# A depthwise convolution stage regrouped: eight channels per tile, shared zero gaps between images, kernel rows in a ring of their own

## The chip, the cores and the metric

The kernel runs on one core of a Trainium2 chip. The metric is the device time of one execution in microseconds (us). All data is float32.

## The reference

Four layers work one after the other on a batch of 8 images with 384 channels and 32 x 32 pixels. The first two are Mamba blocks (projections, a short convolution, a recurrent scan, a gate), the second with a pooled attention gate and a two-layer perceptron behind it. The last two are what this change is about:

```python
# layer 2: seven depthwise convolutions (13x13, and smaller ones, some dilated), each with a batch norm, summed
out = bn_eval(dwconv(x, w_lk, 1), ...)
for i, (w, r) in enumerate(zip(branch_ws, dilates)):
    out = out + bn_eval(dwconv(x, w, r), ...)
# layer 3: a pointwise convolution, then a 13x13 depthwise one
y = jnp.einsum('bchw,oc->bohw', x, pw_w)
x_pw = bn(y, pw_g, pw_b, pw_m, pw_v) + x
out = bn(dwconv(x_pw, dwk_w), ...) + bn(x_pw * dw1_w, ...)
return gelu(out, approximate=False)
```

The kernel folds the seven branches of layer 2 into one 13 x 13 kernel per channel, and the two terms at the end of layer 3 into another. So each of the last two layers has one depthwise 13 x 13 convolution over 8 images of 32 x 32 in 384 channels.

## The kernel before, in words

`layers` (lines 224 to 929) computes both Mamba layers and the perceptron. Its order is written out as a plan with a slot for each step, under a manual schedule for all five engines. While it runs, `prepare` folds the convolution kernels and writes them to DRAM as tables `k2` and `k3`, in a form in which each row of a banded matrix is a window of 512 bytes into a longer line of padded kernel values. The perceptron leaves its result in the DRAM tensor `x3`: `mlp_out` (line 714) adds bias and residual into the tile `rows_out`, whose rows have zeros around the 32 pixels, and `mlp_store` (line 721) stores it, 128 channels at a time.

The tail then has three stages, `conv.run` on `x3`, `point.run` and `conv.run` again (lines 1078 to 1084). Here the scheduler of the framework places the instructions in program order on each engine, and adds the waits.

`Depthwise` does a convolution as matmuls with banded matrices. A group is 4 channels; there are 96 groups in a convolution. The 128 partitions of the image tile `xp` are 4 blocks of 32 image rows: the block number is a shift of the row by 0, 1, 2 or 3 columns. A row holds the 8 images side by side, each with 6 zeros to its left and 6 to its right (WIDE = 44, so 352 values). The tile `wt` holds, for each channel, the banded kernel matrices. For each channel, 4 matmuls of 128 x 32 weights by 256 columns (8 images of 32 pixels), each shifted by 4 columns more, sum up the 13 kernel columns. The 4 channels of a group write 4 different blocks of 32 partitions of one PSUM tile `ps`. The trace records two matmuls for each one in the program, so a group is 32 records.

For each group, `run` does the following:

- `load` (line 951) of the group 6 ahead: two image loads on GpSimd's queue (line 958), which bring the unshifted block for two of the channels and the block shifted by 2 for the other two; and four loads of kernel windows (line 962), two on SyncE's queue, one on ScalarE's and one on GpSimd's. There are 8 buffers each of `wt` and `xp`, and a buffer can be loaded again once the matmuls of its last group are done.
- four copies on VectorE, which make the other shifted blocks: line 975 twice (shift by 1), lines 976 and 977 (shift by 2, down and up).
- 16 matmuls (line 982), one activation with the bias on ScalarE (line 987, Identity in the first convolution and Gelu in the second), and the store of the result on ScalarE's queue (line 988).

In the built program every DMA that SyncE or ScalarE issues uses one of eight completion counters in rotation, and waits until the DMA that had the same counter before has landed. Before the change a group issues four of these (three kernel loads and the store), so a store waits for the store of two groups earlier. GpSimd's DMAs have eight counters of their own.

`Pointwise` (line 991) runs 16 steps of 512 columns: it loads `xt`, does 9 matmuls (line 1016), activations, an addition (line 1021), and stores to `x5` (line 1026) through the tiles `q_out`, again with zeros around the pixels.

Of the kernel before, what the change touches and what calls it, by code (L numbers as in the profile page):

```python
# [9 lines left out]
F32 = mybir.dt.float32  # L10
# [6 lines left out]
P = 128  # L17
B = 8
# [7 lines left out]
T = 512  # L26
NU = B * L // T
HW = 32
# [4 lines left out]
HK = 64  # L33
KP = 4
PAD = KS // 2
WIDE = HW + 2 * PAD
NG = C // 4
EPS = 1e-5
PAST = 16100
# [27 lines left out]
class Plan:  # L67
# [3 lines left out]
    def __init__(self):  # L71
        self.slots = {}
# [859 lines left out]
class Depthwise:  # L932
# [3 lines left out]

    NB, AHEAD = 8, 6

    def __init__(self, tc, st):
        nc = self.nc = tc.nc
        self.keep = st.enter_context(tc.tile_pool(name="d_keep", bufs=1, reuse_waits="tile"))
        self.work = st.enter_context(tc.tile_pool(name="d_work", bufs=4, reuse_waits="tile"))
        self.psum = st.enter_context(tc.tile_pool(name="d_ps", bufs=4, space=PSUM, reuse_waits="tile"))
        self.wts = [self.keep.tile([P, 4, HW, KP], F32, name=f"wt{i}") for i in range(self.NB)]
        self.xps = [self.keep.tile([P, 4, B * WIDE], F32, name=f"xp{i}") for i in range(self.NB)]
        for t in self.wts + self.xps:
            nc.gpsimd.memset(t, 0.0)

    def load(self, g, src, table):
        nc, n = self.nc, B * WIDE
        wt, xp = self.wts[g % self.NB], self.xps[g % self.NB]
        for h in range(2):
            rows = bass.AP(
                src.tensor, src.offset + (g * P + 2 * HW * h) * n + 2 * h, [[n, HW], [HW * n, 2], [1, n - 2 * h]]
            )
            nc.gpsimd.dma_start(xp[2 * HW * h : 2 * HW * h + HW, 2 * h : 2 * h + 2, 0 : n - 2 * h], rows)  # L958
        for s, queue in enumerate((nc.sync, nc.scalar, nc.sync, nc.gpsimd)):
            at = table.offset + (16 * g + s) * HK * KP  # L960
            windows = bass.AP(table.tensor, at, [[KP, HW], [4 * HK * KP, 4], [1, HW * KP]])
            queue.dma_start(wt[HW * s : HW * (s + 1)].rearrange("p q r j -> p q (r j)"), windows)  # L962

    def run(self, src, table, bias, func, store):
        nc = self.nc
        n = B * WIDE
        for g in range(self.AHEAD):
            self.load(g, src, table)
        for g in range(NG):
            wt, xp = self.wts[g % self.NB], self.xps[g % self.NB]  # L970
            if g + self.AHEAD < NG:
                self.load(g + self.AHEAD, src, table)
            for h in range(2):
                low, q = 2 * HW * h, slice(2 * h, 2 * h + 2)
                nc.vector.tensor_copy(xp[low + HW : low + 2 * HW, q, 0 : n - 1], xp[low : low + HW, q, 1:n])  # L975
            nc.vector.tensor_copy(xp[2 * HW :, 0:2, 0 : n - 2], xp[: 2 * HW, 0:2, 2:n])
            nc.vector.tensor_copy(xp[: 2 * HW, 2:4, 2:n], xp[2 * HW :, 2:4, 0 : n - 2])  # L977
            ps = self.psum.tile([P, T], F32, tag="ps", name="ps")
            x = xp.rearrange("p q (b c) -> p q b c", c=WIDE)
            for j in range(KP):  # L980
                for q in range(4):
                    nc.tensor.matmul(  # L982
                        ps[HW * q : HW * (q + 1), : B * HW], wt[:, q, :, j], x[:, q, :, 4 * j : 4 * j + HW],
                        start=j == 0, stop=j == KP - 1,
                    )
            o = self.work.tile([P, B, HW], F32, tag="o", name="o")
            nc.scalar.activation(o, ps[:, : B * HW], func, bias=bias[:, g : g + 1])
            nc.scalar.dma_start(store(g), o)


class Pointwise:


    NB = 3
# [37 lines left out]
def network(ctx: ExitStack, tc: tile.TileContext, a: dict, out: bass.AP):  # L1032
    nc = tc.nc
# [27 lines left out]
    x4 = dram.tile([C, HW * B * HW], F32, name="x4")  # L1061
# [3 lines left out]
    got = {"b2": const.tile([P, NG], F32, name="b2"), "b3": const.tile([P, NG], F32, name="b3")}  # L1065
# [3 lines left out]
    with ExitStack() as st:  # L1069

        past = st.enter_context(tc.tile_pool(name="past", bufs=1, reuse_waits="tile"))
        past.tile([P, PAST], F32, name="past")
        past_ps = st.enter_context(tc.tile_pool(name="past_ps", bufs=1, space=PSUM, reuse_waits="tile"))
        past_ps.tile([P, 4 * T], F32, name="past_ps")
        conv = Depthwise(tc, st)
        point = Pointwise(tc, st, conv.psum, a["pw"])
        x4_rows = x4.rearrange("c (r n) -> (c r) n", r=HW)
# [120 lines left out]
```

## Time and profile before

| what | value |
|---|---|
| median of 3 runs | 6941.13 us (6929.37 to 6941.44) |
| time of the profiled execution | 6954.78 us |
| span of its trace | 6952.9 us |
| mean granted TensorE clock | 0.926 |
| PE busy | 5904.4 us (85%) |
| VectorE busy | 5851.6 us (84%) |
| ScalarE busy | 4475.0 us (64%) |
| GpSimd busy | 5429.7 us (78%) |
| DMA, over the span | 1169.60 MB, mean 168 GB/s |

In the trace, times run from the span's start. The layers take it up to 6373 us, when the last `rows_out` is done. The first depthwise convolution then runs until 6595 us, the pointwise stage until 6732 us (its last store has landed), and the second convolution to the end at 6952.9 us. So what the change edits is some 580 us out of 6953 us, one twelfth.

Views used below: the table of busy time by stretches of the span gives, for each engine, busy time and in brackets the number of records, then the granted clock, the DMA share and the DMA rate. The DMA share is the mean busy share of the core's 16 DMA engines, summed over packets, so it can pass 1 where packets overlap. The table of instruction groups gives line, engine, operation, tiles, shapes and count, then busy time and the mean time in ns of one, then the idle time before them and what ended it. The table of waits says which instruction waited for which, in total, how often, and at most.

### The profile page before, as it was taken

The page shows a single profiled execution, that of the slowest core. Times are in us where ns is not written, and L with a number is a line of the kernel's source. Part 1 is how long each engine was busy: PE and PEld are TensorE (multiplying, and loading weights), DVE is VectorE, ACT ScalarE, POOL GpSimd, SP SyncE. Part 2 cuts the span into 40 slices and gives each one's busy share as a digit, 9 for nine tenths or more (in the row PEclk, how much of TensorE's full clock was granted, in tenths as well). Part 3 has the DMA queues.
Part 4 walks back from the last instruction along what each step waited for, and adds up shares of the span by engine and source line. Part 5 has one row for each costly group of instructions (what it writes and reads, how often), then busy time and mean ns, then how long its engine had stood idle before and what let it go on. Part 6 is the DMA issues. An engine that isn't in the chain of part 4 may idle for free. (4 is left out here: it accounts for less than half of the span.)

```text
span 6952.9 us, 78464 instructions
## 1 busy us (share of the span) xinstructions
PE 5904.4 (85%) x22562; PEld 2097.6 (30%) x22562; DVE 5851.6 (84%) x4975; ACT 4475.0 (64%) x7478; POOL 5429.7 (78%) x3146
## 2 busy tenths in 40 slices
PE   6777788888888888888888888888889889877898
PEld 2222222222322232222222232223223223324645
DVE  2899998999889888888889988988888998863849
ACT  4776666767676767767676767676677667742222
POOL 2888888888788878888888878887877888754626
PEclk7888898999999999999999999999999889999999
DMA  4665555666666566666666665656666666645979
GB/s 123 166 176 155 154 160 149 167 168 173 171 165 181 157 169 167 161 168 167 167 165 172 167 174 161 176 155 174 165 157 168 160 171 172 161 108 131 264 224 242
DMA packets 960565, 1169.60 MB, mean 168 GB/s; under 512 B 314057, under 2 KB 552713, under 8 KB 960137
## 3 DMA queue, kind: packets, MB, share of 16 engines
q1 hardware_dynamic: 787848, 1062.39, 57.5%
q10 hardware_dynamic: 147712, 55.08, 3.1%
q0 software_dynamic: 24576, 47.12, 2.3%
q8 instruction: 184, 3.01, 0.2%
q14 instruction: 245, 2.00, 0.1%
HBM read 909.39 MB, written 204.21 MB: 160 GB/s over the span
## 5 line engine op out<-in xcount | busy, mean ns | idle before, releaser
L532 POOL TENSOR_TENSOR dbu<-B,ru 128x1024 f32<-128x1024 f32 x1536 | 3584.9, 2357 | 136.9 <-DMA B<-bc 56.8
L525 ACT ACTIVATE h<-rd,A 128x512 f32<-128x512 f32 x3072 | 2117.5, 691 | 861.8 <-DVE hc L561 524.8
L553 DVE TENSOR_TENSOR_SCAN h<-h,state,dbu 128x512 f32<-128x512 f32 x1152 | 1482.4, 1287 | 221.1 <-ACT h L525 79.6
L561 DVE TENSOR_TENSOR hc<-h,C 128x1024 f32<-128x1024 f32 x1152 | 1410.8, 1225 | 129.2 <-PE acc L583 14.5
L556 DVE TENSOR_TENSOR_SCAN h<-h,dbu 128x1024 f32<-128x1024 f32 x576 | 1318.1, 2288 | 239.0 <-ACT h L525 182.4
L572 POOL TENSOR_TENSOR hc<-dbu,C 128x1024 f32<-128x1024 f32 x384 | 903.5, 2353 | 736.7 <-DVE dbu L556 337.1
L583 PE MATMUL acc<-hc,fold 128*32 128x512 f32 x6144 | 1174.6, 663 | 340.7 <-DVE hc L561 257.9
L415 PE MATMUL mm<-xt,wi 128*128 128x512 f32 x2232 | 1123.3, 642 | 43.6 <-ACT delta L491 18.9
L695 PE MATMUL f<-mx,wi 128*128 128x512 f32 x1152 | 610.5, 638 | 139.9 <-ACT fh L699 111.0
L708 PE MATMUL f<-fh,wo 128*128 128x512 f32 x1152 | 587.0, 628 | 82.0 <-DMA wo<-in_fc_dram 66.8
L415 PEld LDWEIGHTS mm<-xt,wi 128*128 128x128 f32 x2232 | 424.7, 202 | 745.4 <-issue 447.8
L604 PE MATMUL mm<-u,wo 128*128 128x512 f32 x1152 | 579.4, 643 | 38.5 <-DMA wo<-in_l_out_dram 31.4
L583 PEld LDWEIGHTS acc<-hc,fold 128*32 128x32 f32 x6144 | 165.9, 112 | 1163.7 <-DVE hc L561 548.5
L553 DVE TENSOR_TENSOR_SCAN dbu<-h,state,dbu 128x512 f32<-128x512 f32 x384 | 470.4, 1267 | 14.0 <-ACT h L525 8.6
L556 DVE TENSOR_TENSOR_SCAN dbu<-h,dbu 128x1024 f32<-128x1024 f32 x192 | 437.9, 2281 | 39.8 <-ACT h L525 29.3
L439 PE MATMUL mm<-xp,taps 128*64 128x512 f32 x1536 | 407.0, 653 | 33.8 <-DMA xp<-xp 12.4
L982 PE MATMUL ps<-xp,wt 128*32 128x256 f32 x6144 | 376.1, 387 | 66.0 <-DVE xp L977 30.3
L958 POOL DMA_DIRECT2D xp<-x x384 | 215.4, 565 | 276.8 <-DMA x<-q_out 139.8
L305 ACT ACT_TABLE_LOAD x289 | 370.8, 1283 | 5.9 <-PEq L1186 0.7
L695 PEld LDWEIGHTS f<-mx,wi 128*128 128x128 f32 x1152 | 209.3, 196 | 499.4 <-issue 248.5
L580 PE MATMUL acc<-u,skip 128*128 128x512 f32 x384 | 226.8, 675 | 153.7 <-DVE u L588 153.5
L425 ACT ACTIVATE xp<-mm,b_in 64x512 f32<-64x512 f32 x384 | 261.5, 681 | 140.8 <-PE mm L415 138.3
(152 smaller groups left out, 5876.2 us busy)
## 6 DMA issues: line engine op xcount, KB each, us to landing
ru<-uu SPq DMA_DIRECT2D x1536, 128.0 KB
rd<-dd SPq DMA_DIRECT2D x1536, 128.0 KB
wi<-w_in SPq DMA_DIRECT2D x372, 192.0 KB
xp<-xp SPq DMA_DIRECT2D x384, 128.5 KB
dd<-delta SPq DMA_DIRECT2D x192, 256.0 KB
uu<-delta SPq DMA_DIRECT2D x192, 256.0 KB
wo<-in_l_out_dram SPq DMA_DIRECT2D x96, 384.0 KB
wi<-fc_w SPq DMA_DIRECT2D x192, 192.0 KB
```

Source lines behind the costliest of these rows:

```text
L415: nc.tensor.matmul(s.ps[m], w[:, c], s.xt[:, c], start=c == 0, stop=c == KC - 1)
L439: nc.tensor.matmul(s.ps[d][64 * h : 64 * h + 64], taps[:, h, j], xp[h][:, 2 * j : 2 * j + T], start=j == 0, stop=j == 1,)
L525: nc.scalar.activation(y[:, q], s.dr[d][1][h][:, q], AF.Exp, scale=s.layer.A[:, at : at + 1])
L532: nc.gpsimd.tensor_tensor(dbu, s.B[g].unsqueeze(1).to_broadcast([P, 2, T]), s.ur[d][1][h], ALU.mult)
L553: nc.vector.tensor_tensor_scan(to[:, q], y[:, q], dbu[:, q], first, ALU.mult, ALU.add)
L556: nc.vector.tensor_tensor_scan(flat_to, flat_y, flat_b, first, ALU.mult, ALU.add)
L561: nc.vector.tensor_tensor(hc, to, s.C[g].unsqueeze(1).to_broadcast([P, 2, T]), ALU.mult)
L572: nc.gpsimd.tensor_tensor(hc, y, s.C[g].unsqueeze(1).to_broadcast([P, 2, T]), ALU.mult)
L583: nc.tensor.matmul(s.acc[d][32 * r : 32 * r + 32], k["fold"], tiles[r // 2][:, r % 2], start=False, stop=n == PER - 2)
L604: nc.tensor.matmul(s.ps[m], w[:, d], s.us[d], start=d == 0, stop=d == KD - 1)
L695: nc.tensor.matmul(s.ps[m], s.w["in", m][:, c], s.xt[:, c], start=c == 0, stop=c == KC - 1)
L708: nc.tensor.matmul(s.down, s.w["out", 2 * m + f // KD][:, f % KD], s.hs[f], start=f == 0, stop=f == KF - 1)
```

## The change

- A group is 8 channels, and a convolution has 48 groups. `xp` is 128 x 8 rows, with 4 buffers instead of 8, loaded 3 groups ahead instead of 6. Each group still has two image loads and four VectorE copies, now over 4 channels each instead of 2.
- Two images share one gap of 6 zeros (WIDE = 38, so a row has 304 values instead of 352), and 12 zeros stand behind the last image. `x3`, `x5`, `rows_out` and `q_out` shrink with it.
- `wt` is 128 x 8 x 128 values in a ring of its own with 11 buffers. The first 10 groups of each convolution are loaded by `early`, all on GpSimd's queue: for the first convolution right after the image tiles have been zeroed, for the second right after the first convolution. In the loop, the group 10 ahead is loaded, on SyncE (three of the four loads) and ScalarE (one).
- The zeroing of `wt` goes.
- Each group has two PSUM tiles, each with 16 matmuls, an activation and a store as before. The number of matmuls, activations and stores does not change.

```diff
-WIDE = HW + 2 * PAD
+WIDE = HW + PAD
...
-    NB, AHEAD = 8, 6
+    N2 = NG // 2
+    NB, AHEAD = 4, 3
+    NK, EARLY = 11, 10
...
-        self.wts = [self.keep.tile([P, 4, HW, KP], F32, name=f"wt{i}") for i in range(self.NB)]
-        self.xps = [self.keep.tile([P, 4, B * WIDE], F32, name=f"xp{i}") for i in range(self.NB)]
-        for t in self.wts + self.xps:
+        self.wts = [self.keep.tile([P, 8, HW, KP], F32, name=f"wt{i}") for i in range(self.NK)]
+        self.xps = [self.keep.tile([P, 8, B * WIDE + 2 * PAD], F32, name=f"xp{i}") for i in range(self.NB)]
+        for t in self.xps:
             nc.gpsimd.memset(t, 0.0)
-    def load(self, g, src, table):
+    def kernels(self, g, table, queues):
+        wt = self.wts[g % self.NK]
+        for s, queue in enumerate(queues):
+            at = table.offset + (32 * g + s) * HK * KP
+            windows = bass.AP(table.tensor, at, [[KP, HW], [4 * HK * KP, 8], [1, HW * KP]])
+            queue.dma_start(wt[HW * s : HW * (s + 1)].rearrange("p q r j -> p q (r j)"), windows)
+    def early(self, table):
+        for g in range(self.EARLY):
+            self.kernels(g, table, [self.nc.gpsimd] * 4)
+    def images(self, g, src):
         nc, n = self.nc, B * WIDE
-        wt, xp = self.wts[g % self.NB], self.xps[g % self.NB]
+        xp = self.xps[g % self.NB]
         for h in range(2):
             rows = bass.AP(
-                src.tensor, src.offset + (g * P + 2 * HW * h) * n + 2 * h, [[n, HW], [HW * n, 2], [1, n - 2 * h]]
+                src.tensor, src.offset + (2 * g * P + 4 * HW * h) * n + 2 * h, [[n, HW], [HW * n, 4], [1, n - 2 * h]]
             )
-            nc.gpsimd.dma_start(xp[2 * HW * h : 2 * HW * h + HW, 2 * h : 2 * h + 2, 0 : n - 2 * h], rows)
-        for s, queue in enumerate((nc.sync, nc.scalar, nc.sync, nc.gpsimd)):
-            ...
+            nc.gpsimd.dma_start(xp[2 * HW * h : 2 * HW * h + HW, 4 * h : 4 * h + 4, 0 : n - 2 * h], rows)
     def run(self, src, table, bias, func, store):
         for g in range(self.AHEAD):
-            self.load(g, src, table)
-        for g in range(NG):
+            self.images(g, src)
+        for g in range(self.N2):
-            if g + self.AHEAD < NG:
-                self.load(g + self.AHEAD, src, table)
+            if g + self.AHEAD < self.N2:
+                self.images(g + self.AHEAD, src)
+            if g + self.EARLY < self.N2:
+                self.kernels(g + self.EARLY, table, (nc.sync, nc.scalar, nc.sync, nc.sync))
             for h in range(2):
-                low, q = 2 * HW * h, slice(2 * h, 2 * h + 2)
+                low, q = 2 * HW * h, slice(4 * h, 4 * h + 4)
                 nc.vector.tensor_copy(xp[low + HW : low + 2 * HW, q, 0 : n - 1], xp[low : low + HW, q, 1:n])
-            nc.vector.tensor_copy(xp[2 * HW :, 0:2, 0 : n - 2], xp[: 2 * HW, 0:2, 2:n])
-            nc.vector.tensor_copy(xp[: 2 * HW, 2:4, 2:n], xp[2 * HW :, 2:4, 0 : n - 2])
-            ps = self.psum.tile([P, T], F32, tag="ps", name="ps")
-            ...
+            nc.vector.tensor_copy(xp[2 * HW :, 0:4, 0 : n - 2], xp[: 2 * HW, 0:4, 2:n])
+            nc.vector.tensor_copy(xp[: 2 * HW, 4:8, 2:n], xp[2 * HW :, 4:8, 0 : n - 2])
+            for a in range(2):
+                ps = self.psum.tile([P, T], F32, tag="ps", name="ps")
+                ...
+                nc.scalar.activation(o, ps[:, : B * HW], func, bias=bias[:, 2 * g + a : 2 * g + a + 1])
+                nc.scalar.dma_start(store(2 * g + a), o)
...
         conv = Depthwise(tc, st)
+        conv.early(got["k2"])
         point = Pointwise(tc, st, conv.psum, a["pw"])
         conv.run(
             x3, got["k2"], got["b2"], AF.Identity,
...
+        conv.early(got["k3"])
         point.run(x4, x5, got["pw"][:, 0:KC], got["pw"][:, KC:])
```

In the built program before and after, the instructions of `layers` stand in the same order; only the stores from `rows_out` are smaller. On ScalarE's queue in the loop, the kernel load of a group stands between the second activation of a group and its store.

More of the change, by code (lines that the diff above doesn't have):

```diff
@@ L945, in __init__ @@
         self.psum = st.enter_context(tc.tile_pool(name="d_ps", bufs=4, space=PSUM, reuse_waits="tile"))
-        self.wts = [self.keep.tile([P, 4, HW, KP], F32, name=f"wt{i}") for i in range(self.NB)]
-        self.xps = [self.keep.tile([P, 4, B * WIDE], F32, name=f"xp{i}") for i in range(self.NB)]
-        for t in self.wts + self.xps:
+        self.wts = [self.keep.tile([P, 8, HW, KP], F32, name=f"wt{i}") for i in range(self.NK)]
+        self.xps = [self.keep.tile([P, 8, B * WIDE + 2 * PAD], F32, name=f"xp{i}") for i in range(self.NB)]
+        for t in self.xps:
             nc.gpsimd.memset(t, 0.0)
-    def load(self, g, src, table):
+    def kernels(self, g, table, queues):
[8 more added lines that the diff above has]
+    def images(self, g, src):
         nc, n = self.nc, B * WIDE
-        wt, xp = self.wts[g % self.NB], self.xps[g % self.NB]
+        xp = self.xps[g % self.NB]
         for h in range(2):
             rows = bass.AP(
-                src.tensor, src.offset + (g * P + 2 * HW * h) * n + 2 * h, [[n, HW], [HW * n, 2], [1, n - 2 * h]]
+                src.tensor, src.offset + (2 * g * P + 4 * HW * h) * n + 2 * h, [[n, HW], [HW * n, 4], [1, n - 2 * h]]
             )
-            nc.gpsimd.dma_start(xp[2 * HW * h : 2 * HW * h + HW, 2 * h : 2 * h + 2, 0 : n - 2 * h], rows)
-        for s, queue in enumerate((nc.sync, nc.scalar, nc.sync, nc.gpsimd)):
-            at = table.offset + (16 * g + s) * HK * KP
-            windows = bass.AP(table.tensor, at, [[KP, HW], [4 * HK * KP, 4], [1, HW * KP]])
-            queue.dma_start(wt[HW * s : HW * (s + 1)].rearrange("p q r j -> p q (r j)"), windows)
+            nc.gpsimd.dma_start(xp[2 * HW * h : 2 * HW * h + HW, 4 * h : 4 * h + 4, 0 : n - 2 * h], rows)
     def run(self, src, table, bias, func, store):
@@ L967, in run @@
         for g in range(self.AHEAD):
-            self.load(g, src, table)
-        for g in range(NG):
-            wt, xp = self.wts[g % self.NB], self.xps[g % self.NB]
-            if g + self.AHEAD < NG:
-                self.load(g + self.AHEAD, src, table)
+            self.images(g, src)
+        for g in range(self.N2):
+            wt, xp = self.wts[g % self.NK], self.xps[g % self.NB]
+            if g + self.AHEAD < self.N2:
+                self.images(g + self.AHEAD, src)
+            if g + self.EARLY < self.N2:
+                self.kernels(g + self.EARLY, table, (nc.sync, nc.scalar, nc.sync, nc.sync))
@@ L979, in run @@
[L979 to L987, printed above, removed]
@@ L988, in run @@
-            nc.scalar.dma_start(store(g), o)
+            nc.vector.tensor_copy(xp[2 * HW :, 0:4, 0 : n - 2], xp[: 2 * HW, 0:4, 2:n])
+            nc.vector.tensor_copy(xp[: 2 * HW, 4:8, 2:n], xp[2 * HW :, 4:8, 0 : n - 2])
+            for a in range(2):
+                ps = self.psum.tile([P, T], F32, tag="ps", name="ps")
+                for j in range(KP):
+                    x = xp[:, :, 4 * j : 4 * j + n].rearrange("p q (b c) -> p q b c", c=WIDE)
+                    for q in range(4):
+                        c = 4 * a + q
+                        nc.tensor.matmul(
+                            ps[HW * q : HW * (q + 1), : B * HW], wt[:, c, :, j], x[:, c, :, 0:HW],
+                            start=j == 0, stop=j == KP - 1,
+                        )
+                o = self.work.tile([P, B, HW], F32, tag="o", name="o")
+                nc.scalar.activation(o, ps[:, : B * HW], func, bias=bias[:, 2 * g + a : 2 * g + a + 1])
+                nc.scalar.dma_start(store(2 * g + a), o)
@@ L1075, in network @@
         conv = Depthwise(tc, st)
+        x4_rows = x4.rearrange("c (r n) -> (c r) n", r=HW)
+        conv.early(got["k2"])
         point = Pointwise(tc, st, conv.psum, a["pw"])
-        x4_rows = x4.rearrange("c (r n) -> (c r) n", r=HW)
         conv.run(
```

## The prediction

> **What bounds the tail now.** I read the table of busy time by stretches first, to separate the stages:
>
> ```profile
> core 0: us, PE busy (x) PEld busy (x) DVE busy (x) ACT busy (x) POOL busy (x), PEclk, DMA share, GB/s
> 6500.00:6540.00 40.00, 36.24 (x610) 27.91 (x601) 37.65 (x73) 9.02 (x19) 32.47 (x57) 1.00 0.95 272
> ...
> 6640.00:6690.00 50.00, 50.00 (x118) 22.09 (x117) 13.17 (x19) 15.29 (x20) 0.00 (x0) 1.00 0.72 237
> ...
> 6860.00:6900.00 40.00, 35.37 (x580) 21.01 (x576) 37.65 (x73) 8.54 (x18) 30.09 (x54) 1.00 1.08 257
> ```
>
> In both convolutions (first and last line) VectorE does 73 copies in 40 us, one every 0.548 us: busy 94% of the time, the rest being the gap of 0.03 us between copies. The DMA share is about 1 there too. The pointwise stage (middle) is bound by TensorE. The groups on VectorE in the first convolution (busy us, mean ns of one, idle before them):
>
> ```profile
> L975 DVE COPY xp<-xp 32x702 f32<-32x702 f32 x192 | 99.9, 520 | 9.1 <-PE ps L982 3.1
> L977 DVE COPY xp<-xp 64x700 f32<-64x700 f32 x96 | 50.2, 523 | 3.3
> L976 DVE COPY xp<-xp 64x700 f32<-64x700 f32 x96 | 50.1, 522 | 3.3
> ```
>
> 384 copies of 702 or 700 values with almost no idle time: 4 x 0.548 = 2.19 us for 4 channels, 96 times 210 us. In the timeline they run from 6373.28 to 6589.1 (215.8 us), in the second convolution from 6734.08 to 6946.9 (212.8 us). TensorE's 13 us of idle time at 6372 cost nothing, since the copies run meanwhile. How fast TensorE is when nothing holds it up, finer stretches show (its own busy time, records, clock, DMA share, GB/s):
>
> ```profile
> 6392.00:6394.00 2.00, 2.00 (x44) 1.00 1.05 297
> 6394.00:6396.00 2.00, 2.00 (x45) 1.00 0.89 235
> 6396.00:6398.00 2.00, 2.00 (x44) 1.00 0.77 191
> ```
>
> 44 records in 2 us, so 32 records, a group, in 1.45 us. There VectorE had run some groups ahead. This rate doesn't last; the waits of 6395 to 6510 (total us, times, longest) and the chain of waits from 6395 on say why:
>
> ```profile
> ACT o L987 <- DMA x<-o: 56.1, 37, 3.8
> PEld ps L982 <- ACT o L987: 24.8, 32, 2.0
> ```
>
> ```profile
> 6398.17 5.30 DMA x<-o
> ...
> 6403.55 3.97 DMA x<-o
> ...
> 6407.59 5.27 DMA x<-o
> ```
>
> TensorE waits for PSUM, ScalarE for its stores, and each store for the landing of the one two groups before. The 28 links from 6395.3 to 6515.6 take 4.30 us on average for two groups, 2.15 us per group. So a second bound, the landing of DMAs, lies right beside VectorE's 2.19. Who fills the DMA engines in 6400 to 6590 (packets, MB, share) is the last view:
>
> ```profile
> q0 software_dynamic: 10952, 21.01, 38.7%
> q10 hardware_dynamic: 25884, 17.69, 30.2%
> q1 hardware_dynamic: 26046, 11.86, 24.9%
> ```
>
> q1 (SyncE) carries half of the kernel windows, q10 (ScalarE) a quarter and the stores, q0 (GpSimd) a quarter and the images. All windows thus take 2 x 24.9 = 49.8%, images 38.7 - 12.45 = 26.2%, stores 17.8%. The same view of 6740 to 6940 gives 22.7%, 49.0% and 36.1%: windows 45.4, images 24.8, stores (128 bytes a piece) 37.6, in all 108%.
>
> **What the Trainium skill says.** "VectorE: DVE Perf Modes", the side-by-side table: a float32 copy within SBUF whose outer dimension is even moves 2 values per cycle at 0.96 GHz, after some 150 cycles of fixed cost. For 702 values that is (351 + 8 + 150)/0.96 = 530 ns; the trace has 520, so the fixed part is real and the mode is on. "DMA: Bandwidth & Descriptors", section "Issuing engines are not separate DMA queues": issuing elsewhere only saves issue time. The shares above, which add up to about 1, agree; moving windows from GpSimd to SyncE makes no bandwidth. Same page, "Anatomy of one DMA": 2.0 us plus bytes/436e3, 2.2 us for an image load of 88 KB. The trace has 2.3 with idle engines (6732 to 6736) and 4.3 in the convolution, so about 2 us of queueing: the engines are loaded.
>
> **The change part by part.**
>
> VectorE: 4 copies of 1212 or 1208 values per 8 channels. Fixed part 520 - 351/0.96 = 154 ns; 606/0.96 + 154 = 785 ns (estimate; in proportion to size, the upper bound, 900). With the gap, 4 x 0.815 = 3.26 us instead of 2 x 2.19 = 4.38; upper bound 3.72. Alone this gives 48 x 3.26 = 156.5 us per convolution.
>
> TensorE: the same matmuls, 2 x 1.45 = 2.91 us per 8 channels; under 3.26, so it doesn't bind.
>
> DMA: per 8 channels the windows stay (524 KB, 1024 pieces), stores stay (262 KB), images go from 359 to 310 KB (minus 13.6%). The share before, 0.967 in 6420 to 6540, is 0.967 x 4.38 = 4.23 us of full DMA per 8 channels; images are 26.2/94.7 of it, so 13.6% less makes 4.07. In the second convolution 1.09 x 4.38 = 4.77, less 3%: 4.63. What share can be had? In stretches of 3 us the first convolution reaches at most 1.07, the second 1.21, and in a tenth and a fifth of the stretches they are at 1.05 and 1.15 or above. I take these two: 4.07/1.05 = 3.88 us and 4.63/1.15 = 4.02 us per 8 channels. Both are over 3.26, so DMA becomes the bound while windows are loaded: for 38 of 48 groups, since 10 are loaded early. For the last 10 groups, only images and stores remain (about half the DMA work), and VectorE's 3.26 holds.
>
> First convolution: 38 x 3.88 + 10 x 3.26 = 180.0 us, against 215.8: -35.8. Second: 38 x 4.02 + 32.6 = 185.4, against 212.8: -27.4.
>
> Early loads for the first convolution: 40 DMAs of 131 KB on GpSimd, after zeroing (four tiles of 2528 columns, 2.2 us each by the 1.22 us of 1408 columns; the zeroing of wt, 3.79 us, goes) and ahead of the zeroing of q_out and of the image loads, which wait for x3 until 6360. GpSimd has nothing else from 6308 to 6360, and 40 x 0.56 us of issue is 22 us. The engines are at 0.2 to 0.3 from 6300 to 6330 and idle in 6330 to 6350, so 5.2 MB fit. If they didn't, they would delay the perceptron's weights: 0 to 3 us; I take 1.
>
> Early loads for the second: GpSimd waits for each ring buffer, so they start some 10 us before the first convolution's end, and some 3.7 MB run beside the first pointwise loads. TensorE waited 8.8 us for the first xt there, of which 4.7 is the load; at half the bandwidth about 2 us are added. Later steps have three buffers and a DMA share of 0.7; hidden. So +2.
>
> Image loads: twice as long, now 3 groups of 8 ahead with 4 buffers. A buffer is free when its matmuls end, and is needed 3 groups later. With 3.26 us per group there are about 6.5 us for a landing that takes 4.3 now, and at 3.9 more. Cost 0, up to 0.3 us per group at landings of 8 us.
>
> ScalarE: the window load ahead of a store queues that store, and all later activations, behind a counter that another landing must free. The counters now serve 6 DMAs per 8 channels instead of 8, so the chain of landings allows 0.75 x 4.30 = 3.2 us per group where landings stay as long, and 3.9 where they take 5.2. No cost beside the DMA bound. Smaller x5 stores save under 0.5 us, the longer copies before the first matmul cost about as much: 0.
>
> Sum: -35.8 - 27.4 + 1 + 2 = -60.2 us. The profiled execution (6954.8) would come to 6894.6; it stands 13.7 us above the median, and the saving lies in stages that both have, so I take it off the median: 6941.1 - 60.2 = 6880.9.
>
> **The rivals.**
>
> VectorE stays the bound (share can rise further). For: GB/s reached 313 to 338 in short stretches, 1097 KB in 3.26 us are 336. Against: that rate was never held for 10 us. Then 2 x 156.5 + some 4 us of stalls: -112 + 3, about 6832.
>
> DMA gives no more than its mean today, 269 and 257 GB/s. 1097 KB take 4.08 and 4.27 us: 187.6 and 194.9 us, so -46 + 3: 6898. For: ScalarE already waits for landings in both.
>
> Slower: landings of the doubled window loads. The eight counters let at most 8 such DMAs fly; if a landing takes L, a group takes 0.75 L. Slower from 38 x 0.75 L + 32.6 = 214, so L = 6.4 us, 1.5 times today's link. At L = 7 (5.25 us per group) both convolutions take 232 us: +36 + 3, about 6980. For: windows of 131 KB in place of 64. Against: total bytes don't rise, and stores keep their size.
>
> **How the numbers follow.** DMA as bound, between today's mean rates and shares somewhat above mine, 6855 to 6910: 0.62. VectorE as bound or nearly: 0.20. Between 6910 and 6927, gains partly lost to stalls: 0.05. Within 0.2% of 6941, which is what a measurement can tell: 0.05. Slower: 0.08. So faster 0.87. The range 6832 to 6922 leaves out the last two and the edges.
>
> **What would show it.** Copies at 785 ns; idle time of VectorE between them, ended by image landings or matmuls, in the first 38 groups, and hardly any in the last 10; DMA share 1.05 and 1.15; convolutions of 180 and 185 us; the first xt some 2 us later. Wrong if VectorE never idles (then 6832), if ScalarE waits for landings over 6 us, or if the perceptron's end moves from 6373 by over 5 us.

## The result, and the profile after

The changed kernel takes 6906.26 us (median of 5, 6902.73 to 6914.4) against 6941.13 (median of 5): 34.9 us less, where the sum gave 60.2. The ratio on record for these runs is 0.9958, with an interval of 0.9946 to 0.9969, which is a gain of some 29 us (22 to 37). Two repeats, each beside other runs of the kernel before, gained 26.9 and 18.8 us between the medians. So it is faster, as forecast, and the time lies in the range; but the gain is about half of the sum, and 34.9 is the best of three. The profiled execution took 6903.45 us, with a span of 6901.6 us.

First the table of busy time by stretches, for two stretches of the first convolution and one of the second:

```profile
core 0: us, PE busy (x) PEld busy (x) DVE busy (x) ACT busy (x) POOL busy (x), PEclk, DMA share, GB/s
6400.00:6440.00 40.00, 38.07 (x700) 30.19 (x695) 37.59 (x47) 9.46 (x20) 13.61 (x22) 1.00 1.04 276
...
6480.00:6520.00 40.00, 36.71 (x664) 25.14 (x660) 32.48 (x42) 9.57 (x21) 16.29 (x22) 1.00 1.04 281
...
6820.00:6860.00 40.00, 34.36 (x600) 22.26 (x596) 29.88 (x39) 8.92 (x19) 14.95 (x19) 1.00 1.13 247
```

VectorE has gone from 73 to 47, then 42 copies in 40 us in the first convolution, each for twice the channels: a group of eight channels takes 4 x 40 / 47 = 3.40 us at first and 3.81 later. In the second there are 39 copies, 4.10 us per group. In the last two of these stretches VectorE idles for a fifth and a quarter of the time, so it no longer is the bound. TensorE is busy 92% to 95% of the two stretches of the first convolution; how near it is to its own limit there is worked out below. One of VectorE's three groups of copies in the first convolution (busy us, mean ns of one, idle before them):

```profile
L988 DVE COPY xp<-xp 32x1212 f32<-32x1212 f32 x96 | 77.5, 807 | 16.2 <-DMA xp<-x 11.9 <-PE ps L997 1.6
```

The copy takes the forecast 785 ns: the median of line 988 is 784, and the mean is higher because some take up to 882. The waits of 6400 to 6520 (total us, times, longest) say who holds up whom:

```profile
POOL xp L973 <- PE ps L997: 54.2, 44, 2.9
ACT o L1002 <- DMA wt<-k_rows: 41.8, 20, 3.6
ACT o L1002 <- DMA x<-o: 21.6, 19, 3.5
ACT o L1002 <- PE ps L997: 20.9, 13, 3.4
PEld ps L997 <- ACT o L1002: 12.3, 14, 2.3
```

ScalarE waits for landings of kernel windows and stores 63 us out of 120. Before, it was 72 us in the same stretch, 60 of them for stores. An activation reads no window, so what it stands behind is ScalarE's own queue: a window load or a store that cannot be issued until its counter is free. TensorE waits for nothing but ScalarE, which empties PSUM for it. GpSimd, which issues the image loads, waits for TensorE to free a buffer. The chain of waits of 6395 to 6520 is made of landings again, of windows for 56% and of stores for 14% of its time, where before it was nearly all stores (start, us):

```profile
6438.93 5.01 DMA wt<-k_rows
6443.96 6.28 DMA wt<-k_rows
6450.26 5.68 DMA wt<-k_rows
...
6456.90 4.40 DMA x<-o
```

And the queues in 6740 to 6880 of the second convolution (packets, MB, share):

```profile
q10 hardware_dynamic: 75450, 12.32, 53.1%
q1 hardware_dynamic: 22084, 10.65, 32.5%
q0 software_dynamic: 3088, 10.01, 23.6%
```

In all 110%, with two small queues for instructions. The 70351 packets under 512 bytes in that stretch are nearly all stores of 128 bytes a piece.

By stages, in the profiled executions, with the matmuls' end as the end of a convolution: the first took 178.7 us (217.8 before), the first `xt` was awaited for 13.5 us (8.8), the second convolution took 207.5 us to the end of the span (218.8). From the layers' end to the end of the span it is 534.8 us instead of 579.6: a gain of 44.8. The medians show 10 us less than that. So there are two gaps to explain: 15 us in the stages that the change was to speed up, and 10 us in the layers, which it was not to touch.

### The profile page after: what moved, and what is told of

Its sections match the earlier page's. It is cut to its first block, busy times and chain, and to the rows that moved or that the text cites. A ratio compares the mean times of both kernels' runs of the same rounds, so it can differ in the third digit from the quotient of the medians.

```text
span 6901.6 us, 76776 instructions
## 1 busy us (share of the span) xinstructions
PE 5854.2 (85%) x22562; PEld 2074.2 (30%) x22562; DVE 5757.2 (83%) x4591; ACT 4475.7 (65%) x7478; POOL 5276.5 (76%) x2830
## 5 line engine op out<-in xcount | busy, mean ns | idle before, releaser
L973 POOL DMA_DIRECT2D xp<-x x192 | 127.2, 663 | 390.6 <-PE ps L997 179.6
L997 PE MATMUL ps<-xp,wt 128*32 128x256 f32 x6144 | 346.3, 383 | 44.6 <-ACT o L1002 31.0
```

## The experiments

All kernels in one table. Stages are in us, from the profiled execution. "After layers" is the span after the end of the last `rows_out`. "Layers" is the median minus 1.83 us (time outside the span) minus "after layers", and of that the difference to the kernel before beside which it ran (whose two profiles give 579.6 and 578.8 after the layers; 579.2 is used). This takes the profiled stages for typical ones. "Waits" is the sum, over 1420 to 6350 us, of all waits of the five engines for a DMA.

| kernel | ratio to before | conv 1 | first xt | conv 2 | after layers | layers | waits |
|---|---|---|---|---|---|---|---|
| before | 1 | 217.8 | 8.8 | 218.8 | 579.6 | 0 | 405 |
| before_again | (one run) | 216.6 | 8.0 | 219.0 | 578.8 | | 373 |
| wide_only | 1.0012 [1.0005, 1.0019] | 210.7 | 11.1 | 216.4 | 573.1 | +14.4 | 413 |
| changed | 0.9958 [0.9946, 0.9969] | 178.7 | 13.5 | 207.5 | 534.8 | +9.5 | 449 |
| after_again | 0.9961 [0.9949, 0.9974] | 181.3 | 16.4 | 201.6 | 534.1 | +18.1 | 459 |
| after_chip | 0.9974 [0.9965, 0.9982] | 176.2 | 14.0 | 201.9 | 526.8 | +33.5 | 505 |
| win_pool | 0.9947 [0.9933, 0.996] | 174.6 | 14.2 | 197.6 | 522.9 | +17.7 | 437 |
| win_sync | 1.0025 [1.0016, 1.0034] | 206.2 | 14.3 | 226.3 | 581.6 | +11.9 | 482 |
| late_k3 | 0.9938 [0.9926, 0.995] | 173.5 | 8.6 | 202.3 | 519.8 | +17.1 | 431 |
| rows_store | 0.9933 [0.992, 0.9946] | 176.0 | 15.7 | 180.3 | 507.6 | +21.2 | 439 |
| two_pool_late | 0.9934 [0.9918, 0.9949] | 169.6 | 8.8 | 201.1 | 515.0 | +16.5 | 450 |
| short_ring | 1.0013 [1.0004, 1.0022] | 199.7 | 9.6 | 220.2 | 565.2 | +21.8 | 498 |
| wide44_late | 0.9953 [0.9939, 0.9966] | 178.9 | 10.1 | 212.0 | 537.0 | +5.2 | 388 |
| wide40_late | 0.992 [0.9907, 0.9934] | 177.4 | 8.8 | 208.7 | 529.8 | -10.8 | 380 |
| wide40 | 0.9937 [0.9923, 0.995] | 174.6 | 14.6 | 204.1 | 527.5 | +5.0 | 417 |
| wide40_deep | 0.9926 [0.9913, 0.9939] | 173.8 | 11.7 | 203.7 | 525.1 | +2.9 | 397 |
| wide40_o8 | 0.992 [0.9908, 0.9933] | 170.7 | 9.4 | 204.1 | 519.4 | +3.2 | 367 |

**How far the numbers carry: the same two kernels again.** No edit.

> The changed kernel once more, to see how far the layers ahead of the tail vary from run to run. If the layers' end is only noise, it moves by some us (6367 in the profile of the change, 6373 in that before) while the tail keeps its lengths: first convolution 180 us from the first copy to the last matmul, wait for the first xt 13.5, second convolution 207 us from the first copy to the end. If the change slows the layers, they end later than before on the median.

> The kernel before once more, for a second profile. Its profiled execution was 13.7 us above its median. If that excess lay in the layers ahead of the tail, they end some 10 us earlier than 6373 here, and the tail is again 580 us (217.8 us from first copy to last matmul, 8.8 us to the first pointwise matmul, 218.8 us from the first copy of the second convolution to the end). Then the gain of the tail in the profile, 45 us, is partly given back in the layers. If the layers end at 6373 again, they do not differ.

> The changed kernel once more, on the chip of the three others of this call, so that wide40 can be set against it directly. Both theories: ratio to the kernel before 0.996, waits for DMAs in the layers 430 to 460 us.

The changed kernel gave 0.9961 and, with the last group of runs, 0.9974. Its first convolution repeats within 5 us (176 to 181), its second is 202 in both repeats, so the 207.5 of the first profile is on the high side. In the second profile of the kernel before, the layers end at 6360.9 instead of 6373.3, and the stages after them keep their length, as expected: so the first profile's excess of 13.7 us over its median lay in the layers. The layers differ most, and that has a reason of its own, below.

**What bounds the first convolution: which queue the windows are loaded on.** My theory at this point was that it is the landing of DMAs on shared completion counters that holds the loop, and not the time of the DMA engines; the rivals were full DMA engines, and ScalarE held up by its own window load.

```diff
 # win_pool
-                self.kernels(g + self.EARLY, table, (nc.sync, nc.scalar, nc.sync, nc.sync))
+                self.kernels(g + self.EARLY, table, (nc.sync, nc.gpsimd, nc.sync, nc.sync))
 # win_sync
+                self.kernels(g + self.EARLY, table, (nc.sync, nc.sync, nc.sync, nc.sync))
```

> The window load that ScalarE issues in the loop goes to GpSimd's queue. Same bytes, same pieces; five instead of six DMAs per group use the eight shared counters. Theory 1 (the DMA engines' time per piece is the bound): both convolutions within 3 us of 180 and 207. Theory 2 (the landings behind eight counters are the bound): a group takes 5/8 instead of 6/8 of a landing, so the 38 groups with windows fall to VectorE's 3.26 us or near, some 15 us less in each convolution, about 30 in all. Theory 3 (ScalarE stuck behind its own window load): ScalarE's 83 us of waiting for windows goes, and the waits of TensorE for ScalarE (83 us of weight loads and matmuls) shrink by half: 10 to 20 us in all.

> The window load that ScalarE issues in the loop goes to SyncE's queue, so SyncE issues all four. Bytes, pieces and the six DMAs per group on the shared counters stay; only ScalarE no longer stands behind a window load. Theory 1 and theory 2: no change, within 3 us in each convolution. Theory 3 (ScalarE stuck behind its own window load): 10 to 20 us less in all, as in the run with GpSimd.

Both take the window load off ScalarE. After the layers, win_pool is 4 to 12 us faster than the three profiles of the change, where theory 2 had forecast 30; win_sync is 47 to 55 us slower, which none of the three theories had. The first convolution of win_pool, same bytes in the same pieces:

```profile
6440.00:6480.00 40.00, 40.00 (x740) 27.99 (x736) 35.87 (x46) 11.56 (x25) 23.22 (x35) 1.00 1.09 320
```

320 GB/s, where the change had 269 to 281 in three such stretches of its first profile and at most 290 in those of its repeats: the DMA engines could do more. In win_sync the mean of 6400 to 6520 falls to 257 GB/s, and SyncE's queue from 6420 to 6520 shows why:

```profile
SPq L959 <- DMA x<-o: 55.9, 40, 3.5
```

The window loads on SyncE wait 40 times for a store that ScalarE issued. The tiles have nothing to do with each other; they share a counter. The ring of windows runs dry, and TensorE waits for windows (6400 to 6600), which it never does in the profile of the change:

```profile
PE ps L997 <- DMA wt<-k_rows: 19.3, 9, 5.0
```

In the changed kernel SyncE waits for counters too (6380 to 6600):

```profile
SPq L959 <- DMA wt<-k_rows: 58.4, 46, 3.6
SPq L959 <- DMA x<-o: 57.3, 50, 3.8
...
SPq L959 <- PE ps L997: 2.0, 5, 0.8
```

It waits for a free ring buffer only 2.0 us, and in the timeline it issues windows until 6540.0, while the last copy ends at 6539.95. But the ring has enough in reserve, so these waits cost TensorE nothing. What costs it time is ScalarE, behind its own window loads and stores. So waits for shared counters are shown, in both queues. Whether ScalarE's window load or its stores matter more is not. win_sync takes the window load away, and TensorE's weight loads then wait for ScalarE only 4.6 us in the whole convolution instead of 12.3; but with the ring dry ScalarE is no longer what they wait for first, so this doesn't decide it. The gain of win_pool in the first convolution, 2 to 7 us, is hardly more than the 5 us between repeats.

How much there was to win, TensorE's own pace shows. The prediction read it from 44 records in 2 us. But a record lasts 0.38 us, and a stretch counts each record that touches it. The prediction's three stretches of 2 us have 44, 45 and 44 records, 133 in all; the 6 us that they make up have 118, in the same trace of the kernel before:

```profile
6392.00:6398.00 6.00, 6.00 (x118) 5.98 (x114) 3.75 (x8) 0.95 (x2) 4.74 (x10) 1.00 0.90 241
```

So 4 us more bring 74 records more, 18.5 in a us, and the 64 records of a group of eight channels take 3.46 us and not 2.91. A stretch of two_pool_late (below), in which TensorE is never idle, gives the same, 706 records for 38 us more:

```profile
6440.00:6480.00 40.00, 40.00 (x750) 36.18 (x742) 36.13 (x47) 10.94 (x24) 34.42 (x47) 1.00 1.08 318
```

In all 17 profiles, from the start of a record to the start of the 64th after it, the least is 3.45 us. That is more than VectorE's 3.26. 48 groups at 3.45 take 166 us. Taken from each record to the 64th after it, 74% of the first convolution of the change is within 1% of this pace (two_pool_late: 96%), of its second 30%. So after the change TensorE is the main bound of the first convolution. Of its 178.7 us, 1.7 pass before the first matmul, and some 11 are what the landings cost. 1097 KB per 3.45 us are 318 GB/s, so the rates of two_pool_late are TensorE's pace and those of win_pool come near it: they are no limit of the DMA engines.

**The depth of the ring.**

```diff
-    NK, EARLY = 11, 10
+    NK, EARLY = 4, 3
```

> The changed kernel with a ring of four kernel rows and three loaded early, as deep as the images' own, instead of eleven and ten. If the ring's depth carries the gain: seven more groups of each convolution go at the pace with windows, 7 x (3.6 to 3.9 - 3.3) = 2 to 4 us each, and windows issued three groups (11 us) ahead run out whenever SyncE waits for a counter: convolutions 185 and 212 us or more, 6920. If eight channels per instruction carry it and the depth is only reserve: 12 early loads in place of 40 shorten the wait for the first xt from 13.5-16 to about 9 and the early loads of the first convolution by 1 to 2, against 4 to 8 lost: 6903 to 6910, ratio 0.9955.

The convolutions take 199.7 and 220.2 us, well over the 185 and 212 us that the first expectation names as the least: with a ring no deeper than before, counted in channels, the rest of the change is worth 17 us in the first convolution and nothing in the second. The depth carries most of the gain. Late windows are paid from the ring's reserve, and three groups of reserve are not enough: TensorE waits for windows 16 us in the first convolution.

**The early loads of the second convolution.** In late_k3 they are spread over the pointwise steps 3 to 12, on SyncE, one group a step.

```diff
-        conv.early(got["k3"])
 ...
+            if 3 <= i < 3 + conv.EARLY:
+                conv.kernels(i - 3, table, [nc.sync] * 4)
```

> The ten early groups of the second convolution are loaded on SyncE's queue, one group after each of the pointwise steps 3 to 12, instead of on GpSimd's at the end of the first convolution. If they collide with the first xt, its wait falls from 13.5 to the 8.8 us of the kernel before: 4 to 5 us less in all. If the wait has another cause (ScalarE's last stores), it stays at 13 us. The second convolution stays at 207 us in both cases.

The wait of TensorE for the first `xt`, in the change and in late_k3:

```profile
PE ps L1031 <- DMA xt<-x: 13.5, 1, 13.5
```

```profile
PE ps L1033 <- DMA xt<-x: 8.6, 1, 8.6
```

8.6 is what the kernel before had (8.8). So these loads cost 5 to 8 us at the pointwise stage's start (13.5, 16.4 and 14.0 us in the three profiles of the change). The first convolution is shorter too, 173.5 instead of 176 to 181 us. That this comes of the early loads is not shown: in the change the first of them is issued at 6511.0, and by the copies of group 38, shortly before, late_k3 is already 1 to 4 us ahead.

**What bounds the second convolution: the pieces of the stores.** rows_store writes the results in rows of 1024 bytes to a scratch tensor instead of 128-byte pieces to the output; only the last tile goes to the output, so the rest of it is left out.

```diff
-        conv.run(x5, ..., lambda g: out_rows[g * P : (g + 1) * P])
+        conv.run(x5, ..., lambda g: out_rows[g * P : (g + 1) * P] if g == NG - 1
+                 else x6[g * P : (g + 1) * P].rearrange("p (b w) -> p b w", w=HW))
```

> The second convolution stores rows of 1024 bytes to a scratch tensor, as the first does, and only the last store goes to the output: the output is left out but for that. Theory 1 (time per piece in the DMA engines) and any theory in which landings get shorter with fewer pieces: the second convolution becomes like the first, 180 us to the last matmul and about 187 to the end instead of 202 to 207. If the 128-byte pieces cost nothing, it stays at 202 to 207.

The second convolution falls from 202 to 207 us to 180.3, and to the last matmul it takes 176.2, like the first; 88% of its records now stand within 1% of TensorE's pace. The stretch and the queues (6740 to 6850) of rows_store:

```profile
6740.00:6780.00 40.00, 40.00 (x748) 30.03 (x744) 38.45 (x48) 10.04 (x22) 12.67 (x23) 1.00 1.04 291
```

```profile
q10 hardware_dynamic: 16519, 11.56, 38.1%
q1 hardware_dynamic: 20273, 9.78, 35.9%
q0 software_dynamic: 2864, 9.25, 27.9%
```

These are more bytes on ScalarE's queue in less time of the engines than with 128-byte pieces in the same stretch of the change:

```profile
q10 hardware_dynamic: 58826, 9.84, 53.7%
q1 hardware_dynamic: 17071, 8.23, 32.3%
q0 software_dynamic: 2397, 7.76, 23.4%
```

**Both together, and what else might hold the second convolution.** two_pool_late has half of the windows on GpSimd and the late loads of late_k3; wide40_deep and wide40_o8 try other reserves, on rows of 40 columns (the next experiment).

```diff
 # two_pool_late, beside the edit of late_k3
+                self.kernels(g + self.EARLY, table, (nc.sync, nc.gpsimd, nc.sync, nc.gpsimd))
 # wide40_deep, beside those of two_pool_late and WIDE = HW + 8
+    NB, AHEAD = 5, 4
+    NK, EARLY = 8, 7
 # wide40_o8, beside those of two_pool_late and WIDE = HW + 8
-        self.work = st.enter_context(tc.tile_pool(name="d_work", bufs=4, reuse_waits="tile"))
+        self.work = st.enter_context(tc.tile_pool(name="d_work", bufs=8, reuse_waits="tile"))
+    NK, EARLY = 10, 9
```

> Two of the four window loads of a group on GpSimd's queue, two on SyncE's, none on ScalarE's, and the early groups of the second convolution after the pointwise steps 3 to 12. Four DMAs per group on the shared counters instead of six, as in the kernel before per 8 channels half of its eight. Theory 2 (counters): a group is bound by VectorE, 3.3 to 3.5 us with GpSimd's issue beside it, so 165 to 172 us in the first convolution; with the xt wait at 8.8 us. In all 20 to 30 us less than the changed kernel, about 6880. Theory 1 (time per piece): 175 and 200 us as in the run with one load on GpSimd.

> wide40_late with five image tiles loaded four groups ahead instead of four and three, and for want of memory a ring of eight rows with seven early. In the second convolution VectorE waited 41 us for images to land. If the lead of the images is what makes it late: those waits fall to under 20 us and the second convolution from about 205 to 195, in all 10 us less than wide40_late, ratio 0.9905. If the DMA engines are full there (busy 0.9 or more in nearly every slice of it, 41% of it with the stores' 128-byte packets): no shorter second convolution, and the shorter ring costs up to 5 us: ratio 0.992 to 0.9925.

> wide40_late with eight output tiles instead of four (and a ring of ten rows, nine early). In the second convolution of wide40_late ScalarE waits 75 us, 46 times, for its own stores to land, and TensorE for ScalarE. If it is the four tiles that make ScalarE wait: those waits go, and the second convolution is 10 to 15 us shorter: ratio 0.990. If they are waits for a shared counter or for full DMA engines: the same as wide40_late within 4 us, 0.992.

In two_pool_late the first convolution comes down to 169.6 us at 305 to 318 GB/s, inside the 165 to 172 of theory 2, but for another reason than VectorE: it is at TensorE's pace. The second stays at 201, theory 1's number. In it, ScalarE's waits (6687 to 6888) are for its own stores:

```profile
ACT o L1002 <- DMA out_dram<-o: 74.5, 47, 4.8
```

The other two are set against wide40_late, whose second convolution takes 208.7 us. Twice as many output tiles make it 204.1, image loads one group further ahead 203.7: no more than the 5 us between repeats. With eight tiles ScalarE's 75 us of waits for its stores are gone from the table, but TensorE still waits for ScalarE; so the tiles do not limit it. With the images further ahead VectorE waits for them 31 us instead of 41, where under 20 was expected, so the lead isn't cleared as well as the tiles are. What shortened the second convolution by over 20 us was only rows_store, that is, the size of the pieces, and with it the tensor that they go to. That the pieces cost through the engines' time and not through the counters is likely, since windows on GpSimd's own counters gave 4 us at most against the repeats; the two were not separated further, since larger pieces also land sooner.

**The layers: the shared gap alone, and other widths.** wide_only is the kernel before with rows of 38 columns, with the tile size and the slices that such rows need, and nothing else of the change.

```diff
 # wide_only, on the kernel before
-WIDE = HW + 2 * PAD
+WIDE = HW + PAD
 # wide44_late, on two_pool_late (and NK, EARLY = 9, 8)
+WIDE = HW + 2 * PAD
 # wide40_late, on two_pool_late, and wide40, on the changed kernel
+WIDE = HW + 8
```

> The kernel before with WIDE = 38 alone: 4 channels per group, old buffers and queues. Copies of 606 and 604 values: 303/0.96 + 154 = 470 ns, 4 x 0.50 = 2.0 us per group instead of 2.19, 192 us per convolution if VectorE stays the bound. The landings (4.30 us for two groups, 2.15 us per group) don't get shorter: theory 2 (counters) gives 2.1 to 2.15 us per group, 5 to 8 us less in each convolution; VectorE alone would give 18 us less in each.

> two_pool_late with the old row of 44 columns instead of 38 (and, for want of memory, a ring of nine rows and eight early). Seen so far: in the two profiles of the kernel before, waits for DMAs in the layers between 1420 and 6350 us sum to 405 and 373 us; in the seven profiles with 38 columns they sum to 413 to 459, and the layers end some 10 to 15 us later once the medians are set against the stages. Theory A: the layers' 48 stores of rows_out, now in pieces of 152 instead of 176 bytes, cost that time. Then here the waits come back to 370 to 405 us and the layers end at about 6358; the convolutions' copies rise to 154 + 4 x 351 / 1.92 = 885 ns, 3.6 us per group, so that the stages after the layers take 525 to 535 instead of 515: 6885 to 6895, ratio 0.993. Theory B: the layers differ by chance or through the place of the conv code: waits stay at 430 to 460, layers at 6372, 6900 to 6910, ratio 0.995.

> two_pool_late with rows of 40 columns (a shared gap of eight), so that the layers store pieces of 160 bytes, a multiple of 32 as 176 is of 16; 152 is a multiple of 8 only. Theory A1 (the start and size of the pieces count): waits for DMAs in the layers fall to 370 to 405 us, the layers end near 6358, the stages after them take about 519 (copies 823 ns): 6879, ratio 0.992. Theory A2 (short pieces cost, whatever their place): in between, 6885. Theory B (nothing to do with the pieces): 6372 + 519 + 2 = 6893, ratio 0.994, waits 430 to 460.

> The changed kernel with one edit: rows of 40 columns (a shared gap of eight zeros) instead of 38. Seen: waits for DMAs between 1420 and 6350 us are 372 to 405 us with 44 or 40 columns in four profiles of five (388 and 380 in the last two), and 413 to 459 with 38; in the 8 us after each store of rows_out the DMA engines are busy 0.80 to 0.83 of the time with 40 or 44 columns and 0.87 to 0.89 with 38. Theory A (pieces of 152 bytes, a multiple of 8, are what costs; 160 and 176 are multiples of 16): 10 to 15 us faster than the changed kernel on the same chip, ratio to the kernel before 0.994 against 0.996, waits below 405. Theory B (the layers differ from build to build by something else, as short_ring's late end of the layers at 6400 us hints): the same as the changed kernel within 5 us, or slower by the longer copies.

wide_only saves 6 us after the layers (6 to 7 in the first convolution, 2 to 3 in the second, less 2 to 3 at the first `xt`), where theory 2 had 5 to 8 in each convolution, and is 8 us slower in all. wide44_late's layers are near those of before, as theory A has it, but its convolutions, with longer copies, more bytes and a shorter ring, take 20 us more than two_pool_late's, so that it is slower than expected. Beside one another, wide40 has a median of 6896.81 us and the unedited change 6924.66 (6914.1 to 6938.53), 28 us apart where theory A had 10 to 15, with the same stages after the layers (527.5 and 526.8). In the column "layers", the ten rows with 38 columns stand at +9.5 to +33.5 us and the five edited ones with 40 or 44 at -10.8 to +5.2: no overlap. Not all of the 28 us need be the stores' own. The mean granted clock was 0.9252 in the 12 runs of this repeat of the change, 0.9290 in the 5 of wide40, and in four sets of runs of the kernel before a clock lower by 0.001 goes with 0.6 to 3.4 us more; so 2 to 13 of them could go with the clock, and whether the longer waits lower it or it differs by itself is open. The sums of waits overlap a little (wide40's 417 is over the 405 that I had expected at most), but differ in the same way. The loss comes from places such as this one, behind the store of `rows_out` at 5395; the changed kernel (start, us, instruction, idle time before and what ended it):

```profile
5412.75 1.42 ACT L525 ACTIVATE h<-rd,A 128x512 f32<-128x512 f32 x2 [7.77 <-DMA rd<-dd]
```

```profile
5416.83 4.53 PE L604 MATMUL mm<-u,wo 128*128 128x512 f32 x6 [8.50 <-DMA wo<-in_l_out_dram]
```

The same two instructions in before_again:

```profile
5412.88 1.42 ACT L525 ACTIVATE h<-rd,A 128x512 f32<-128x512 f32 x2 [3.51 <-DMA rd<-dd]
```

```profile
5416.32 4.51 PE L604 MATMUL mm<-u,wo 128*128 128x512 f32 x6 [3.44 <-DMA wo<-in_l_out_dram]
```

These loads stand behind the store on SyncE's queue. From that store to the next, 465 us later in wide40, the ten 38-column profiles take 7 to 19 us more than wide40, the six others with 40 or 44 columns 1 to 6. In the 8 us that begin 1.5 us after each `rows_out` (48 stretches of one profile), the DMA share is on average 0.79 to 0.85 and the rate 178 to 185 GB/s with 40 or 44 columns (seven profiles), 0.87 to 0.90 and 162 to 169 with 38 (ten profiles). Line 721 stores pieces of one image row: 176 bytes before, 152 in the change, 160 with 40 columns. The queue it stands in, 1420 to 6350 us, in before_again and in wide_only:

```profile
q1 hardware_dynamic: 577249, 801.40, 59.8%
```

```profile
q1 hardware_dynamic: 577136, 798.93, 62.4%
```

Fewer bytes take more time. (The first profile of the kernel before has 61.2% here, wide40 60.7%, the change 62.9%.) Since 160 bytes do not cost what 152 do, it isn't the number of bytes; whether it is where a piece starts (multiples of 8 bytes instead of 16 or 32), its length, or the place of the tensor in memory was not tried apart.

## Why the prediction was right and wrong

- **VectorE.** Right. 785 ns forecast, 784 measured (median of line 988); the bound of 2.19 us per four channels is gone. "VectorE: DVE Perf Modes" (side-by-side table: two values per cycle for a float32 copy with an even outer dimension, on top of a fixed cost) was enough to get this to 1 ns from a row of the old profile. Some copies take up to 899 ns, which the step left out; it costs little, since VectorE idles.
- **"TensorE: 2 x 1.45 = 2.91 us; under 3.26, so it doesn't bind."** This step failed. A group takes TensorE 3.45 us, so it is the next bound after VectorE, and at that pace no convolution takes less than 166 us. The rate was misread, as shown above. That the sum was hardly hurt is luck: DMA was put at 3.88 and 4.02, and only its last ten groups, at 3.26, were out of TensorE's reach. The rival in which VectorE stays the bound, at 156.5 us, was not to be had.
- **First convolution, -35.8.** Measured -39.1 against the same profile (217.8 to 178.7), -36.5 and -41.6 in the repeats: right in size, wrong in its way. The step took DMA engine time as the bound. win_pool and two_pool_late moved the same bytes at 304 and 313 GB/s (means of 6400 to 6520; the change 275), so engine time did not hold it: TensorE did, and on top of that the landings behind shared counters. The sentence of "DMA: Bandwidth & Descriptors" ("Issuing engines are not separate DMA queues") that issuing elsewhere only saves issue time, on which I relied, doesn't hold for this program: other queues for the same window loads gave rates from 257 (win_sync) to 313 GB/s (two_pool_late) in that stretch, and the queue decides which counters are shared.
- **"Only images and stores remain" in the last ten groups** is a step that failed. The windows of the last groups were loaded until the end, the last issued at 6540.0 in the first convolution and 6888.1 in the second. From copy to copy the last ten groups took 3.68 and 4.06 us each instead of 3.26; a pace near 3.26 was had in the first ten instead (3.36 and 3.40), from the full ring.
- **Second convolution, -27.4.** This is the first term that was mis-sized. Measured -11.3, and -17.2 and -16.9 in the repeats. From first to last copy, as the forecast counted, it took 196.2 us instead of 185.4: the 28 groups between the first and the last ten took 4.34 us each where 4.02 was forecast, and the last ten 4.06 where it was 3.26, less what the first ten saved. I took a share of 1.15 as to be had, from the busiest fifth of short stretches; over 6740 to 6880 it was 1.10. On top, from the last copy to the end it took 11.3 us (6890.3 to 6901.6) instead of 6.0, since TensorE now runs behind the copies. rows_store shows that the stores of 128-byte pieces to the output, which the change left as they were, keep this convolution over 20 us longer than rows of 1024 bytes to a scratch tensor do.
- **Early loads, +1 and +2.** The second is mis-sized: +4.7 at the first `xt`, and +7.6 and +5.2 in the repeats. I had seen the collision, but taken half the bandwidth for the loss; late_k3 shows the whole. For the first, a wait of 2.9 us for the weights `wo` of the perceptron stands near the layers' end; what it cost by itself wasn't measured.
- **"I take it off the median", with the layers left as they are.** This step failed, and it is the second part of the gap. Nothing in the order of the layers' instructions changes, but WIDE is also the row length of `rows_out`, and its 48 stores became slower for the loads behind them: +9.5 us in the first comparison, +18.1 and +33.5 in the repeats. The sum has no term for it. The prediction's own test (the perceptron's end moving from 6373 by over 5 us) pointed the wrong way: it came at 6366.8, 6.4 us earlier, because the layers of the first profile had ended 12 us later than those of the second.

Worked out for the first comparison: the forecast of -60.2, with +16.1 for the second convolution, +2.7 for the first `xt`, -3.3 for the first convolution and -0.1 for the rest, gives the -44.8 measured after the layers. The +9.5 of the layers is what then remains to the medians, so that the whole closes by its making; and a stage repeats within some 5 us only.

Of the rivals, the one in which "DMA gives no more than its mean today" came closest in time (6898), but that is luck, as its reason doesn't hold: the rate rose to 278 GB/s in the first convolution (6380 to 6540) and fell to 238 in the second (6740 to 6880). The slower rival, by landings, needed 6.4 us; the links of the chain are mostly 4 to 6 us, and win_sync, where the windows come late, is slower than before by 0.25%.

The best version found is wide40_late: 6884.22 us beside 6944.46, a ratio of 0.992. wide40_o8 (0.992) and wide40_deep (0.9926) can't be told from it. It has rows of 40 columns, half of the windows on GpSimd, and the kernel rows of the second convolution loaded during the pointwise stage.

## What to carry to other kernels

How fast an engine is, read from long stretches, or from the difference of a long and a short one: a short one counts the records at its edges in full. A constant that sets the layout of a tensor reaches into every stage that writes it: look at the pieces of its stores there, not only at their bytes. A ring of early loads helps as a reserve against late landings; don't count on its last groups being free of loads, but ask what the loading queue waits for. And where DMAs of several engines share completion counters, a load can wait for another engine's store: moving it to a queue with counters of its own is worth a trial before the DMA engines are called full.

## What was not expected of the hardware

- Stores in pieces of 152 bytes held up the loads behind them more than those of 160 or 176 bytes (share 0.87 to 0.90 against 0.79 to 0.85 in the 8 us after a store). "DMA: Bandwidth & Descriptors" ("Specifications") names a read-modify-write for all transfers below 512 bytes; it doesn't tell these three sizes apart, and the runs do.
- The packets of the same 128-KB stores took 43% of the DMA engines' time as 128-byte pieces (6740 to 6850: 53.7% of q10 less a third of q1's 32.3%, ScalarE's windows), and 26%, for more of them, as 1024-byte rows (38.1% less a third of 35.9%).
- A DMA share over 1 left room. With the same bytes on other queues a stretch of 40 us went from 269 to 281 GB/s (share 1.02 to 1.04) up to 320 (1.09, win_pool).
- The matmuls of a group of eight channels, 64 records, never took less than 3.45 us in any of the 17 profiles.
